# Context statistics kept for a second layer, and the order of slots in self-attention, in a transformer block on one core

## The chip, the cores and the metric

The kernel runs on one core of a Trainium2 chip. Its engines are TensorE (PE, with weight loads shown apart as PEld), VectorE (DVE), ScalarE (ACT), GpSimd (POOL) and SyncE (SP); SP, ACT and POOL also issue DMAs. The metric is the device time of one execution in microseconds. Everything is float32.

## What is computed

Two layers of a diffusion transformer (B = 8 sequences of N = 512 tokens, width H = 512, 16 heads of 32, a context of S = 77 rows for each sequence, a condition vector for each). Layer 0 is cross-attention with adaptive LayerNorm on both sides; layer 1 is self-attention with modulation, cross-attention to the same context, and an MLP:

```python
def layer_0(x, context, c):
    xq  = ada_ln(x,       c, Wss_q,  bss_q,  eps=1e-5)   # (1 + scale) * LN(x) + bias
    xkv = ada_ln(context, c, Wss_kv, bss_kv, eps=1e-5)
    return x + attention(xq @ Wq + bq, xkv @ Wkv + bkv) @ Wp + bp

def layer_1(x, context, c):
    shift_a, scale_a, gate_a, shift_m, scale_m, gate_m = split(silu(c) @ W_mod + b_mod, 6)
    q, k, v = split(modulate(ln(x), shift_a, scale_a) @ W_qkv + b_qkv, 3)
    x = x + gate_a * (softmax(q @ k.T * scale) @ v @ W_proj + b_proj)
    q_c = ln(x) @ W_qc + b_qc                            # ln: eps=1e-6
    k_c, v_c = split(ln(context) @ W_kvc + b_kvc, 2)
    x = x + softmax(q_c @ k_c.T * scale) @ v_c @ W_cproj + b_cproj
    h = gelu(modulate(ln(x), shift_m, scale_m) @ W_mlp1 + b_mlp1) @ W_mlp2 + b_mlp2
    return x + gate_m * h
```

Both layers normalise the same context rows; the mean and the variance of a row are the same in both, and only eps differs (1e-5 and 1e-6).

## The kernel before, in words

The stages follow each other: a set-up with the condition's modulations and the context's keys and values (0 to about 75 us of the profile), layer 0's cross-attention (tiles with the suffix _x, to about 450), self-attention (_a, to about 1375), layer 1's cross-attention (_c, to about 1750) and the MLP. The products of cross-attention and MLP are done in Strassen's manner, with sums of blocks on DVE and POOL.

**Context.** The 8 x 77 = 616 rows lie in CT = 5 tiles of 128 rows (the last has 104). `context_x` takes bn_stats and bn_aggr for each tile, gets 1/sqrt(var + eps) by a bit trick and Newton steps on DVE (`rsqrt`, L210 to L219), and normalises. For layer 1 the class `ContextC` loads the rows again (`load`), and its generator `norm` takes the statistics again (L428 to L432), then `rsqrt`, then normalises on ACT (L237). `transpose` makes cT_c on PE (L448) with two evacuations on ACT for each of four blocks (L452, L453); `values(t)` makes the value rows of tile t (cv_c, L345, L350) and stores them to DRAM (cvd_c) by SP; `keys(j)` makes ckT_c (L474, L479).

**Set-up.** `mod_half` makes half of a modulation: four matmuls with the silu of the condition, an ACT copy, then four transpositions on PE and an addition of the bias, which lies in a column of bcol. The bias columns come from one transposition of a table of bias rows (bcol_ps), with a copy and three scalings on DVE.

**Self-attention.** 32 groups run one after the other: batch b by fc = 0 to 3, each with four heads. A group's scores are kept transposed (keys on partitions) in four slots k = 0 to 3 of two halves, e[k][0] and e[k][1], each 128 x 1024. The steps of a group:

- `scores(k)`: eight matmuls into two PSUM tiles (sT_a, L992); for each half an ACT copy to e (L1010) and, for k > 0, a DVE maximum into mx (L1012). ACT copies half i while DVE takes the maximum of the other half, so each of them waits for the other's release of PSUM.
- `maxima()`: DVE turns mx in 32 x 32 blocks and reduces (tu_a L1023, part_a L1024, four times).
- `spread()`: PE transposes part (mxT, L1032), DVE reduces and negates (L1036), SP stores the row of maxima to DRAM (mxd).
- `shift(k)`: two DMAs on POOL's queue, 512 KB each, which broadcast mxd over the partitions and add it to e[k] (L1046).
- `exp(k)`: two ACT exponentials (L1055), each when its DMA has landed. `add_up(k)` sums e over k (L1062; on POOL, for k = 3 on DVE). `outputs(k)` multiplies by the values (o_ps, L1072). `total` and `finish` make the softmax's denominator (z_ps, L1083), its reciprocal (rz, L1090) and the product (oT, L1093).

The order is written out by hand in the loop of `self_phase`. Iteration n handles three groups: prev (n − 1), whose last slots are finished, g (n), which is shifted and begun, and nxt (n + 1), whose scores are made. Between them `pump(f[i], ...)` issues projections of the batch before (`project`, L291, followed by DVE's res_a L961 and POOL's L964 and L965), queries, keys and values of this batch or the next. The sequence before is: prev.outputs(1), nxt.scores(0), g.spread, past.total and finish, prev.add_up(2), the eight shifts with prev.exp(3) after the first two, f[0], nxt.scores(1), prev.outputs(2), f[1], nxt.scores(2), prev.add_up(3), prev.outputs(3), g.exp(0), f[2] with nxt.scores(3) in its middle, g.exp(1), g.add_up(1), nxt.maxima, g.outputs(0), f[3], g.exp(2).

In iterations with fc = 2 the next batch's normalised rows are transposed: `transpose_x(b + 1, t)`, t = 0 to 3, four PE transpositions (lnT, L913) and an ACT evacuation with modulation (xnT, L915) each. Before, they stand ahead of prev.outputs(2), behind it, ahead of nxt.scores(2) and behind it. load_x (L901, ACT's queue) loads the rows of the batch after the next.

The last batch (b = 7) has no next one. In its iteration with fc = 1 the context rows are loaded again; with fc = 2 (group 30 is g, group 31 is nxt) `norm` takes its statistics after nxt.scores(1) and its rsqrt after prev.add_up(3); the normalisation, `transpose`, the values and the keys stand in the code behind the loop, among group 31's shift, exponentials and outputs, as do the loads of x_c (the first rows of the next phase, `next_x`), of the gate and of the residual rows (`load_tile`), the statistics of x_c (`rows`), and the last batch's projection.

Of the kernel before, what the change touches and what calls it, by code (L numbers as in the profile page):

```python
# [11 lines left out]
F32 = mybir.dt.float32  # L12
# [17 lines left out]
def tile_pixart_block(ctx: ExitStack, tc: tile.TileContext, a: dict, out: bass.AP):  # L30
# [6 lines left out]
    MC = MLP // P  # L37

# [46 lines left out]

    def mod_half(u, w, bname, dst, pool, psp, tag):
# [8 lines left out]
        mark = nc.scalar.copy(m, ps[:B, :])  # L95
        pt = psp.tile([P, H], F32, tag=tag, name=f"modT_ps_{bname}_{u}")
# [12 lines left out]

    R = B * S  # L110
    CT = -(-R // P)
    RL = R - (CT - 1) * P

# [32 lines left out]
    with tc.tile_pool(name="setup_ps", bufs=2, space=PSUM) as spp:  # L146
# [17 lines left out]

        bp = spp.tile([P, H], F32, tag="ps", name="bcol_ps")
# [8 lines left out]
        w_ss_kv = [load_w("L0_xcond_Wss_kv", u) for u in range(2)]  # L174
        for u in range(2):
            mark = mod_half(u, w_ss_kv[u], "L0_xcond_bss_kv", mod_kv, sp, spp, "ps")
# [119 lines left out]
    def run(gen):  # L296
        while True:
            try:
                next(gen)
            except StopIteration as stop:  # L300
                return stop.value

# [32 lines left out]
    with tc.tile_pool(name="ps_s", bufs=2, space=PSUM, reuse_waits="tile") as ps_s:  # L335
# [17 lines left out]
        def context_x(eps, w_k, w_v, bkv, work, prep, cx):  # L353
# [14 lines left out]
            for k in range(KC):  # L368
# [14 lines left out]
                if k % 2:  # L383
                    mark = mod_half(k // 2, w_ss_q[k // 2], "L0_xcond_bss_q", mod_q, prep, ps_m, "m")
# [20 lines left out]
            return kT, vs, last, mark  # L405

        class ContextC:
# [17 lines left out]
            def norm(self):  # L425

                mv = small.tile([P, CT, 2], F32, tag="cmv", bufs=1, name="cmv_c")
                nc.vector.memset(mv, 1.0)  # L428
                for t, n in enumerate(parts):
                    bn = small.tile([P, 6], F32, tag="st", name=f"cst_c_{t}")  # L430
                    nc.vector.bn_stats(bn[:n], self.cx[t][:n])
# [448 lines left out]
        def self_phase(w, bo_row, work, work_2, ctx_c):  # L880
# [93 lines left out]
            class Group:  # L974
# [78 lines left out]
                def exp(self, k):  # L1053
                    for i in range(2):
# [74 lines left out]
            for n, g in enumerate(groups[:-1]):  # L1129
# [3 lines left out]
                f = beside(b, fc)  # L1133
                if fc == 3:
# [27 lines left out]
                if fc == 3 or (b, fc) == (0, 0) or fc == 2 and not more:  # L1162
# [16 lines left out]
                if fc == 2 and more:  # L1179
                    transpose_x(b + 1, 2)  # L1180
                nxt.scores(2)
                if fc == 2 and more:
# [3 lines left out]
                if prev is not None:  # L1186
                    prev.add_up(3)
                if (b, fc) == (0, 0) or fc == 2 and not more:
                    next(ln)
                if prev is not None:  # L1190
                    prev.outputs(3)
# [38 lines left out]
            run(ctx_c.values(1))  # L1230
# [403 lines left out]
```

## Time and profile before

| | us |
|---|---|
| median of 3 runs | 2559.84 (2558.33 to 2559.86) |
| the profiled execution | 2562.95 |
| its span in the profile | 2561.1 |
| granted TensorE clock, mean | 0.988 of full speed |

Shares of the chain of work that ended last, followed back from the last instruction, by engine:

| engine | share |
|---|---|
| PE | 31% |
| issue (waiting for nothing that the profile shows) | 28% |
| DMA | 15% |
| DVE | 14% |
| POOL | 7% |
| ACT | 4% |

The page cuts the span in 40 slices of 64 us. In the slices of self-attention (from the eighth to the twenty-second) the 16 DMA engines are busy for eight or nine tenths most of the time and move about 180 to 215 GB/s; before and after they are mostly under half busy. POOL's queue (q0), which is nearly all shifts, moves 151 MB, the queues of SP and ACT (q1) 108 MB.

In a line of a group or a timeline, the name left of the arrow is what is written, right of it what is read. Brackets at the end of a timeline line give the time for which the engine had been idle, and what ended it.

### The profile page before, as it was taken

The numbers are of one execution on the slowest core, as the hardware profiler recorded it, in microseconds if no ns is written. First come the engines' busy times: TensorE is split into PE (matmuls) and PEld (weight loads), VectorE is DVE, ScalarE is ACT, GpSimd is POOL, SyncE is SP. The second block draws the span as 40 slices with busy tenths as digits, with TensorE's granted clock in tenths as the row PEclk, the third lists the DMA queues.
The fourth block names the chain that finished last, engine by engine and source line by source line (L and its number), as shares of the span: only waits on it lengthen the run. The fifth ranks groups of instructions, "written<-read, shape, count | busy, mean of one in ns | idle before, by whom it ended". The sixth has DMA issues, their size and how long they took to land.

```text
span 2561.1 us, 35366 instructions
## 1 busy us (share of the span) xinstructions
PE 2431.1 (95%) x13205; PEld 1561.8 (61%) x13205; DVE 1781.2 (70%) x3240; ACT 1222.7 (48%) x2083; POOL 1111.6 (43%) x982
## 2 busy tenths in 40 slices
PE   7899999989999999999969999998999999999998
PEld 3577776323333333333325777777888888888887
DVE  3688886478788787887766788887546545555553
ACT  1566664477676676777643666662121121121220
POOL 2245453276776877768663445445102102012011
PEclk9999999999999999999989999999999999999999
DMA  7324323589999999999985223133111011011010
GB/s 259 134 51 97 85 32 69 111 177 187 197 179 204 185 196 195 183 198 176 216 181 189 79 38 62 23 51 111 35 36 38 31 40 38 25 32 51 19 35 25
DMA packets 116676, 273.44 MB, mean 107 GB/s; under 512 B 12722, under 2 KB 29186, under 8 KB 116378
## 3 DMA queue, kind: packets, MB, share of 16 engines
q0 software_dynamic: 46368, 151.06, 32.8%
q1 hardware_dynamic: 64197, 108.37, 12.6%
q10 hardware_dynamic: 5941, 11.76, 1.3%
q8 instruction: 104, 1.70, 0.3%
q14 instruction: 66, 0.54, 0.1%
HBM read 234.78 MB, written 44.76 MB: 109 GB/s over the span
## 4 chain that ended last, share of the span: by engine, by line
PE 31%; issue 28%; DMA 15%; DVE 14%; POOL 7%; ACT 4%; POOLq 0%; SPq 0%; ACTq 0%; DVEq 0%
DMA e_a<-mxd_a 10%; PE s_ps_qx L511 4%; PE s_ps_qc L511 4%; PE s_ps_ox L511 2%; DVE mx_a L1012 2%; PE s_ps_oc L511 2%; POOL res_m L1543 2%; POOL e_a L1046 2%; DMA mxd_a<-mxT_a 2%; POOL xr L1544 2%; PE pT_ps_c L743 2%; PE pT_ps_x L743 2%; PE proj_ps_a L291 2%; DVE sum_a L1062 2%; DVE tu_a L1023 2%
## 5 line engine op out<-in xcount | busy, mean ns | idle before, releaser
L1543 POOL TENSOR_TENSOR res_m<-res_m,gate_m 128x256 f32<-128x256 f32 x64 | 52.3, 817 | 665.0 <-DVE res_m L1541 665.0
L1055 ACT ACTIVATE e_a<-e_a 128x1024 f32<-128x1024 f32 x256 | 263.4, 1056 | 108.4 <-DMA e_a<-mxd_a 107.8
L1046 POOL DMA_DIRECT2D e_a<-mxd_a x256 | 251.0, 2061 | 146.9 <-DMA mxd_a<-mxT_a 131.7
L1010 ACT COPY e_a<-sT_a 128x1024 f32<-128x1024 f32 x256 | 253.2, 1010 | 90.3 <-DVE mx_a L1012 67.1
L1477 ACT ACTIVATE hT<-hT,bcol 128x512 f32<-128x512 f32 x128 | 91.9, 722 | 237.3 <-DVE hT L1452 229.2
L1062 POOL TENSOR_TENSOR sum_a<-e_a,e_a 128x1024 f32<-128x1024 f32 x64 | 150.2, 2365 | 116.7 <-ACT e_a L1055 111.9
L992 PE MATMUL sT_a<-qT_a,kT_a 32*128 32x512 f32 x1024 | 153.6, 645 | 21.2 <-ACT e_a L1010 19.5
L1062 POOL TENSOR_TENSOR sum_a<-sum_a,e_a 128x1024 f32<-128x1024 f32 x64 | 171.2, 2686 | 2.6 <-ACT e_a L1055 1.8
L1012 DVE TENSOR_TENSOR mx_a<-sT_a,mx_a 128x1024 f32<-128x1024 f32 x128 | 150.4, 1216 | 25.7 <-PE sT_a L992 25.6
L1072 PE MATMUL o_ps_a<-e_a,v 128*32 128x512 f32 x1024 | 146.9, 618 | 13.1 <-ACT e_a L1055 13.0
L1444 PE MATMUL q_ps_h<-x_m,w_L_xcond_W_mlp 128*128 128x256 f32 x512 | 132.1, 381 | 0.0
L1444 PE MATMUL q_ps_h<-xT_m,w_L_xcond_W_mlp 128*128 128x256 f32 x512 | 131.4, 379 | 0.0
L1012 DVE TENSOR_TENSOR mx_a<-sT_a,e_a 128x1024 f32<-128x1024 f32 x64 | 77.8, 1224 | 76.9 <-PE sT_a L992 39.6
L1444 PE MATMUL q_ps_h<-x_m,w_s 128*128 128x256 f32 x512 | 122.3, 382 | 5.5 <-DVE w_s L1398 4.8
L1090 DVE RECIPROCAL rz_a<-z_ps_a 128x512 f32<-128x512 f32 x32 | 107.5, 3358 | 28.2 <-PE z_ps_a L1083 28.2
L291 PE MATMUL proj_ps_a<-w_L_xcond_W_proj,oT_a 128*128 128x512 f32 x256 | 117.6, 604 | 9.3 <-ACT xnT_a L915 9.3
L283 PE MATMUL q_ps_a<-xnT_a,w_L_xcond_W_qkv 128*128 128x512 f32 x256 | 124.1, 613 | 0.0
L283 PE MATMUL k_ps_a<-xnT_a,w_L_xcond_W_qkv 128*128 128x512 f32 x256 | 121.3, 612 | 0.0
L291 PE MATMUL v_ps<-w_L_xcond_W_qkv,xnT_a 128*128 128x512 f32 x256 | 119.7, 611 | 0.0
L992 PEld LDWEIGHTS sT_a<-qT_a,kT_a 32*128 32x128 f32 x1024 | 44.0, 183 | 120.6 <-ACT e_a L1010 55.8
L1444 PE MATMUL q_ps_y<-w_L_xcond_W_mlp,h_s 128*128 128x256 f32 x512 | 113.1, 379 | 0.0
L1444 PE MATMUL q_ps_y<-w_L_xcond_W_mlp,hT 128*128 128x256 f32 x512 | 113.1, 379 | 0.0
(370 smaller groups left out, 5574.6 us busy)
## 6 DMA issues: line engine op xcount, KB each, us to landing
e_a<-mxd_a POOLq DMA_DIRECT2D x256, 512.0 KB, 11.6
xa<-res_x POOLq DMA_DIRECT2D x32, 256.0 KB, 5.2
xr_a<-xa SPq DMA_DIRECT2D x32, 256.0 KB, 4.4
xc<-xr_a SPq DMA_DIRECT2D x32, 256.0 KB, 8.4
x_c<-xc SPq DMA_DIRECT2D x8, 1024.0 KB, 5.1
w_L_xcond_W_mlp<-in_L_xcond_W_mlp_dram SPq DMA_DIRECT2D x8, 1024.0 KB, 6.9
xc<-res_c POOLq DMA_DIRECT2D x32, 256.0 KB, 5.1
x_m<-xc SPq DMA_DIRECT2D x8, 1024.0 KB, 5.2
```

What stands on the lines that cost most here:

```text
L283: nc.tensor.matmul(ps, lhsT=w[:, k, ts(j, P)], rhs=xT[k], start=(k == 0), stop=(k == KC - 1))
L291: nc.tensor.matmul(ps, lhsT=xT[k][:, cols], rhs=w[:, k, :], start=(k == 0), stop=(k == KC - 1))
L511: nc.tensor.matmul(ps, lhsT=self.lhs[i][:, k], rhs=self.rhs[i][:, k], start=(k == 0), stop=(k == 1),)
L992: nc.tensor.matmul(sc[h // 2][:, h % 2, :], lhsT=kT[ts(h, HD), ts(k, P)], rhs=qT[ts(h, HD), :], start=True, stop=True,)
L1010: nc.scalar.copy(self.e[k][i], sc[i])
L1012: nc.vector.tensor_tensor(self.mx[1 - i], sc[1 - i], self.e[0][1 - i] if k == 1 else self.mx[1 - i], ALU.max,)
L1046: nc.gpsimd.dma_start(out=self.e[k][i].rearrange("p h n -> p (h n)"), in_=self.mxd[2 * i : 2 * i + 2, :] .rearrange("h n -> (h n)").partit ...
L1055: nc.scalar.activation(self.e[k][i], self.e[k][i], AF.Exp)
L1062: engine.tensor_tensor(sum_i, self.e[0][i] if k == 1 else sum_i, self.e[k][i], ALU.add)
L1072: nc.tensor.matmul(self.po[ts(h, HD), :], lhsT=vt[:, self.fc * P + h * HD : self.fc * P + (h + 1) * HD], rhs=self.e[k][h // 2][:, h % 2, : ...
L1090: nc.vector.reciprocal(r, self.pz)
L1444: nc.tensor.matmul(self.banks[n][:, half], lhsT=lhsT, rhs=rhs, start=(k == 0), stop=(k == len(pairs) - 1),)
```

## The change

- The mean and variance of the context's rows, as layer 0 took them (`mv`), are handed from `context_x` to `ContextC`, which makes the factor (with eps 1e-6) and the offset from them when it is built, ahead of the self-attention phase: a rsqrt, a copy and an offset on tiles of 128 x 5. The memset, bn_stats, bn_aggr and the rsqrt in the last loop iteration go.
- Two of the five context tiles are normalised after nxt.scores(2) of the last iteration, three after g.exp(1); `transpose` stands at that iteration's end, ahead of the last group's first step.
- Behind the loop the values, the keys, the loads of x_c, gate and residual rows, and x_c's statistics take other places among the last group's slots.
- prev.exp(3) is split: its first half stays, its second half goes behind nxt.scores(1) (and behind the first transposition of a turning iteration).
- The transpositions of a turning iteration take other slots: 0 as before, 1 behind f[1] and ahead of nxt.scores(2), 2 behind these, 3 and load_x behind prev.outputs(3).
- `mod_half` becomes a generator that pauses after its ACT copy; the bias table's transposition, copy and scalings come between the two parts of the first half, and w_ss_kv is loaded ahead of them.

The core of the diff (the moves of `run`, R, CT and RL to an earlier place are left out):

```diff
@@ set-up
+        w_ss_kv = [load_w("L0_xcond_Wss_kv", u) for u in range(2)]
+        halves = [
+            mod_half(u, w_ss_kv[u], "L0_xcond_bss_kv", mod_kv, sp, spp, "ps") for u in range(2)
+        ]
+        next(halves[0])
         bp = spp.tile([P, H], F32, tag="ps", name="bcol_ps")
         nc.tensor.transpose(bp[:, :n_cols], brow, ident[:n_cols, :n_cols])
...
-        for u in range(2):
-            mark = mod_half(u, w_ss_kv[u], "L0_xcond_bss_kv", mod_kv, sp, spp, "ps")
+        run(halves[0])
+        mark = run(halves[1])
@@ class ContextC
-            def __init__(self, w_v, work):
+            def __init__(self, w_v, work, mv):
+                y = rsqrt(mv[:, :, 1], 1e-6, "cc", CT)
+                self.y = small.tile([P, CT], F32, tag="cy", bufs=1, name="cy_c")
+                self.off = small.tile([P, CT], F32, tag="coff", bufs=1, name="coff_c")
+                nc.vector.tensor_copy(self.y, y)
+                nc.vector.scalar_tensor_tensor(self.off, mv[:, :, 0], -1.0, y, ALU.mult, ALU.mult)
...
             def norm(self):
-                mv = small.tile([P, CT, 2], F32, tag="cmv", bufs=1, name="cmv_c")
-                nc.vector.memset(mv, 1.0)
                 for t, n in enumerate(parts):
-                    bn = small.tile([P, 6], F32, tag="st", name=f"cst_c_{t}")
-                    nc.vector.bn_stats(bn[:n], self.cx[t][:n])
-                    nc.vector.bn_aggr(mv[:n, t, :], bn[:n])
-                    if t in (2, CT - 1):
-                        yield
-                y = rsqrt(mv[:, :, 1], 1e-6, "cc", CT)
-                off = offsets(mv, y, CT)
-                yield
-                for t, n in enumerate(parts):
-                    normalise_s(self.cx[t][:n], self.cx[t][:n], off, y, t, n)
+                    normalise_s(self.cx[t][:n], self.cx[t][:n], self.off, self.y, t, n)
+                    yield
@@ the loop of self_phase
+                turning = fc == 2 and more
...
-                    prev.exp(3)
+                    prev.exp(3, [0])
...
                 nxt.scores(1)
-                if fc == 3 or (b, fc) == (0, 0) or fc == 2 and not more:
+                if fc == 3 or (b, fc) == (0, 0):
                     next(ln, None)
                     next(ln, None)
...
-                if fc == 2 and more:
+                if turning:
                     transpose_x(b + 1, 0)
                 if prev is not None:
+                    prev.exp(3, [1])
                     prev.outputs(2)
-                if fc == 2 and more:
-                    transpose_x(b + 1, 1)
...
                 pump(f[1], 4)
...
-                if fc == 2 and more:
-                    transpose_x(b + 1, 2)
+                if turning:
+                    transpose_x(b + 1, 1)
                 nxt.scores(2)
-                if fc == 2 and more:
-                    transpose_x(b + 1, 3)
-                    if b + 2 < B:
-                        load_x(b + 2)
+                if turning:
+                    transpose_x(b + 1, 2)
+                if fc == 2 and not more:
+                    next(ln)
+                    next(ln)
                 if prev is not None:
                     prev.add_up(3)
-                if (b, fc) == (0, 0) or fc == 2 and not more:
+                if (b, fc) == (0, 0):
                     next(ln)
                 if prev is not None:
                     prev.outputs(3)
+                if turning:
+                    transpose_x(b + 1, 3)
+                    if b + 2 < B:
+                        load_x(b + 2)
...
                 g.add_up(1)
+                if fc == 2 and not more:
+                    run(ln)
                 nxt.maxima()
                 g.outputs(0)
                 pump(f[3], 4)
+                if fc == 2 and not more:
+                    ctx_c.transpose()
                 g.exp(2)
@@ behind the loop
-            run(ln)
             prev.outputs(2)
-            ctx_c.transpose()
+            for t in range(2):
+                run(ctx_c.values(t))
             prev.add_up(3)
             prev.outputs(3)
-            run(ctx_c.values(0))
+            value = ctx_c.values(2)
+            next(value)
             prev.total()
+            run(value)
             prev.finish()
...
             next_x(nc.sync)
-            run(ctx_c.values(1))
-            value = None
             rows = ln_rows("c", 0, 1e-6)
+            fills = [ctx_c.values(3), ctx_c.values(4), ctx_c.keys(0)]
             for k in range(NT):
                 g.exp(k)
                 if k:
                     g.add_up(k)
-                    run(value)
                 g.outputs(k)
-                if k == 2:
+                if k == 0:
                     st[g.b]["g"] = gate_rows(gate_a, g.b, work, "a")
-                    for _ in range(4):
-                        next(rows)
                     for t in range(NT):
                         load_tile(B - 1, t, nc.sync)
-                if k + 2 < CT:
-                    value = ctx_c.values(k + 2)
-                    next(value)
-            run(value)
-            run(rows)
+                if k < len(fills):
+                    run(fills[k])
             w_c = [load_w("L1_xcond_W_qc", 0, queue=nc.scalar)]
             w_c.append(load_w("L1_xcond_W_cproj", 0, queue=nc.scalar))
-            run(ctx_c.keys(0))
+            run(ctx_c.keys(1))
             g.total()
             g.finish()
-            run(ctx_c.keys(1))
+            run(rows)
             for t in range(NT):
                 run(project(B - 1, t))
```

More of the change, by code (lines that the diff above doesn't have):

```diff
@@ L37, in tile_pixart_block @@
     MC = MLP // P
+    R = B * S
+    CT = -(-R // P)
+    RL = R - (CT - 1) * P
     const = ctx.enter_context(tc.tile_pool(name="const", bufs=1))
@@ L84, in bias_cols, with run @@
         return bcol[:, c : c + n]
+    def run(gen):
+        while True:
+            try:
+                next(gen)
+            except StopIteration as stop:
+                return stop.value
     def mod_half(u, w, bname, dst, pool, psp, tag):
@@ L108, in mod_half @@
         return mark
-    R = B * S
-    CT = -(-R // P)
-    RL = R - (CT - 1) * P
     def load_context(pool):
@@ L172, in tile_pixart_block @@
             )
-        w_ss_kv = [load_w("L0_xcond_Wss_kv", u) for u in range(2)]
-        for u in range(2):
-            mark = mod_half(u, w_ss_kv[u], "L0_xcond_bss_kv", mod_kv, sp, spp, "ps")
+        run(halves[0])
+        mark = run(halves[1])
         w_ss_q = [load_w("L0_xcond_Wss_q", 0)]
@@ L294, in mm_N @@
             yield
[L296 to L301, printed above, removed]
     def gate_rows(gate, b, pool, nm, bufs=2):
@@ L383, in context_x @@
                 if k % 2:
-                    mark = mod_half(k // 2, w_ss_q[k // 2], "L0_xcond_bss_q", mod_q, prep, ps_m, "m")
+                    mark = run(mod_half(k // 2, w_ss_q[k // 2], "L0_xcond_bss_q", mod_q, prep, ps_m, "m"))
             vd = dram.tile([R, H], F32, name="cvd_x")
@@ L404, in context_x @@
             prep.release()
-            return kT, vs, last, mark
+            return kT, vs, last, mark, mv
         class ContextC:
-            def __init__(self, w_v, work):
+            def __init__(self, w_v, work, mv):
[4 more added lines that the diff above has]
+                nc.vector.scalar_tensor_tensor(self.off, mv[:, :, 0], -1.0, y, ALU.mult, ALU.mult)
                 self.work, self.w_v = work, w_v
@@ L425, in norm @@
             def norm(self):
-                mv = small.tile([P, CT, 2], F32, tag="cmv", bufs=1, name="cmv_c")
-                nc.vector.memset(mv, 1.0)
                 for t, n in enumerate(parts):
-                    bn = small.tile([P, 6], F32, tag="st", name=f"cst_c_{t}")
-                    nc.vector.bn_stats(bn[:n], self.cx[t][:n])
-                    nc.vector.bn_aggr(mv[:n, t, :], bn[:n])
-                    if t in (2, CT - 1):
-                        yield
-                y = rsqrt(mv[:, :, 1], 1e-6, "cc", CT)
-                off = offsets(mv, y, CT)
-                yield
-                for t, n in enumerate(parts):
-                    normalise_s(self.cx[t][:n], self.cx[t][:n], off, y, t, n)
+                    normalise_s(self.cx[t][:n], self.cx[t][:n], self.off, self.y, t, n)
+                    yield
             def transpose(self):
@@ L1051, in shift, with exp @@
                         )
-                def exp(self, k):
-                    for i in range(2):
+                def exp(self, k, halves=(0, 1)):
+                    for i in halves:
                         nc.scalar.activation(self.e[k][i], self.e[k][i], AF.Exp)
@@ L1178, in self_phase @@
                     ln = ctx_c.norm()
-                if fc == 2 and more:
+                if turning:
+                    transpose_x(b + 1, 1)
+                nxt.scores(2)
+                if turning:
                     transpose_x(b + 1, 2)
-                nxt.scores(2)
-                if fc == 2 and more:
+                if fc == 2 and not more:
+                    next(ln)
+                    next(ln)
+                if prev is not None:
+                    prev.add_up(3)
+                if (b, fc) == (0, 0):
+                    next(ln)
+                if prev is not None:
+                    prev.outputs(3)
+                if turning:
                     transpose_x(b + 1, 3)
@@ L1185, in self_phase @@
                         load_x(b + 2)
-                if prev is not None:
-                    prev.add_up(3)
-                if (b, fc) == (0, 0) or fc == 2 and not more:
-                    next(ln)
-                if prev is not None:
-                    prev.outputs(3)
                 flush(0)
@@ L1314, in tile_pixart_block @@
             with tc.manual_schedule(engines={ENG.PE}):
-                kT, vs, last, mark = context_x(1e-5, w_l0[0], w_l0[1], names[1], kv_x, sp, cx)
+                kT, vs, last, mark, c_mv = context_x(1e-5, w_l0[0], w_l0[1], names[1], kv_x, sp, cx)
             stack.enter_context(tc.manual_schedule(engines=ALL_BUT_SYNC))
@@ L1334, in tile_pixart_block @@
             w_l1 = [load_w("L1_xcond_W_qkv", u) for u in (2, 0, 1)] + [load_w("L1_xcond_W_proj", 0)]
-            ctx_c = ContextC(load_w("L1_xcond_W_kvc", 1), work)
+            ctx_c = ContextC(load_w("L1_xcond_W_kvc", 1), work, c_mv)
             w_c, kv = self_phase(w_l1, load_row("L1_xcond_b_proj", 0, "bo"), work, work_2, ctx_c)
```

## The prediction

> **What bounds the kernel now.** I read the page first, then TensorE's and ACT's waits in the self-attention loop, then the engines' shares by stretch, then the timeline at the loop's end.
>
> ```profile
> PE 2431.1 (95%) x13205; PEld 1561.8 (61%) x13205; DVE 1781.2 (70%) x3240; ACT 1222.7 (48%) x2083; POOL 1111.6 (43%) x982
> ...
> L1055 ACT ACTIVATE e_a<-e_a 128x1024 f32<-128x1024 f32 x256 | 263.4, 1056 | 108.4 <-DMA e_a<-mxd_a 107.8
> L1046 POOL DMA_DIRECT2D e_a<-mxd_a x256 | 251.0, 2061 | 146.9 <-DMA mxd_a<-mxT_a 131.7
> ```
>
> TensorE is busy for 95% of the span, so only its 130 us of idle time, and what it does twice, can be won. Much of that idle time is in the self-attention phase (450 to 1375 us). Its waits from 450 to 1350 us (engine, line, what it waited for: us, times, longest):
>
> ```profile
> PE mxT_ps_a L1032 <- DVE part_a L1024: 20.3, 25, 2.7
> PE sT_a L992 <- ACT e_a L1010: 19.5, 17, 4.7
> PE o_ps_a L1072 <- ACT e_a L1055: 13.0, 3, 10.2
> PE proj_ps_a L291 <- ACT xnT_a L915: 9.3, 6, 2.4
> ```
>
> The third is nearly all one wait, at the loop's end; the others are spread over the groups. A turning group (fc 2, where the next batch is transposed) shows the second and fourth kinds: ACT stands in e[3]'s second half until its transfer lands, and the score copies and the evacuation that the projection needs queue up behind it. ACT, then TensorE:
>
> ```profile
> 752.48 1.06 ACT L1055 ACTIVATE e_a<-e_a 128x1024 f32<-128x1024 f32 x1 [1.24 <-DMA e_a<-mxd_a]
> 753.44 1.91 ACT L1010 COPY e_a<-sT_a 128x1024 f32<-128x1024 f32 x2
> ```
> ```profile
> 756.09 3.70 PE L291 MATMUL proj_ps_a<-w_L_xcond_W_proj,oT_a 128*128 128x512 f32 x8 [1.02 <-ACT xnT_a L915]
> ...
> 775.83 0.30 PE L1032 MATMUL mxT_ps_a<-ident,part_a 128*64 128x128 f32 x1 [1.17 <-DVE part_a L1024]
> ```
>
> A second resource stands close behind TensorE. By stretch (length, PE, PEld, DVE, ACT, POOL busy, granted clock, DMA share, GB/s):
>
> ```profile
> 680.00:860.00 180.00, 170.94 (x743) 56.37 (x742) 150.99 (x182) 127.13 (x145) 130.68 (x93) 1.00 0.95 192
> 860.00:1040.00 180.00, 170.62 (x746) 56.89 (x748) 148.39 (x178) 126.53 (x143) 135.92 (x98) 1.00 0.96 195
> ```
>
> PE idles 9 us in 180 (5%), the DMA engines 4 to 5%. Neither can give more than some 40 us over the loop's 790 us. The loop's end, DVE, then PE, then POOL:
>
> ```profile
> 1288.08 0.68 DVE L431 BATCH_NORM_STATS2 cst_c<-cx 128x6 f32<-128x512 f32 x1
> ...
> 1298.26 1.23 DVE L210 TENSOR_SCALAR lnv_cc<-cmv_c 128x5 f32<-128x5 f32 x1
> ...
> 1305.74 2.35 DVE L1012 TENSOR_TENSOR mx_a<-sT_a,mx_a 128x1024 f32<-128x1024 f32 x2
> ```
> ```profile
> 1295.03 1.76 PE L992 MATMUL sT_a<-qT_a,kT_a 32*128 32x512 f32 x8 [4.71 <-ACT e_a L1010]
> ...
> 1309.07 2.87 PE L1072 MATMUL o_ps_a<-e_a,v 128*32 128x512 f32 x8 [10.22 <-ACT e_a L1055]
> 1313.88 0.30 PE L1032 MATMUL mxT_ps_a<-ident,part_a 128*64 128x128 f32 x1 [1.94 <-DVE part_a L1024]
> ```
> ```profile
> 1316.48 1.79 POOL L1046 DMA_DIRECT2D e_a<-mxd_a  x2 [2.69 <-DMA mxd_a<-mxT_a]
> ```
>
> Context statistics hold the scores' maxima of the last group; ACT's score copy waits for those, and the exponentials wait behind the copy: 4.71 + 10.22 + 1.94 us of TensorE.
>
> **Statistics once, and the last slots.** Removed from DVE in the last loop iteration: 1288.08 to 1292.15 = 4.1 us (five bn_stats and bn_aggr) and 1298.26 to 1305.83 = 7.5 us (13 small operations, up to 1.23 us each beside POOL's adds, 0.17 without). So the maxima end up to 11.6 us sooner: mx2 from 1289.1 (sT2 is there then), 2.35 us, the sums 3.4, mx3 2.35, four transposes with reduces 5.7: part ready near 1303 for 1313.9. But the 20 context transpositions now stand ahead of mxT(31) on PE, and their last three inputs are normalised (3 x 0.72 us) after exp(1), whose transfer lands at 1299.57 and which ends near 1300.6; transpositions and eight evacuations take 3.5 us more: about 1306.5 for mxT(31). (The evacuations hold up exp(2), landed at 1304.87, by some 1.6 us; o(30,2) and o(30,3) wait for the last landing anyway.) mxd goes out near 1307, and group 30's transfers drain at 1311.27; so the first shift of group 31 goes from 1316.48 to about 1312, a gain of 4.4 us. TensorE's idle time of 16.9 us isn't the gain: group 31 can't start before the queue of group 30 drains. The rest turns into waiting for that.
> On SP two more value stores (cvd_c1, cvd_c2) now go ahead of x_c0, and the gate and xr loads ahead of cvd_c3; these loads (x_c0 1 MB, four xr rows 1 MB) share some 8 us more of group 31's transfers. From 1330 to 1342, queue 0 moved 1.84 MB beside queue 1's 1.02 (153 KB/us); successive landings without queue 1 (1299.57, 1302.05) give 512 KB in 2.5 us, about 200: 8 x 47/200 = +1.8 us. The stretch 1318 to 1328 without queue 1 shows only 168 KB/us, which makes it +0.7; I take 1.8.
> The Trainium skill ("DMA: Bandwidth & Descriptors", section "Queues, rings and completion order") says that each engine takes the queues in turn, a packet from each; with the 4 KB and 2 KB packets here that is an estimate of two thirds for queue 0, and 8 x 1/3 = +2.7 us in place of +1.8. The row's 153 of 200 is kinder than the rule.
> After the last landing (before: 1345.73) the order saves PE's 2.48 us wait for z at 1354.90, and moves one value block and ckT0 (4.5 us, 1347.85 to 1352.3) under the transfers; x_c's statistics (5.7 us on DVE) go ahead of the residual instead: the end of the projection comes 25.3 us after the landing, for 28.5 (1374.21 − 1345.73): −3.2. Tail: −4.4 + 1.8 − 3.2 = **−5.9** (rounded), between −9 (no sharing) and −2 (mxT late by 4 us more).
>
> **What that adds earlier.** 14 small DVE operations come into the first cross phase near 383 to 388 us, ten ahead of u_qx (L637 at 385.24). Alone 0.17 us, 0.2 apart: 10 x 0.2 = 2 us, less 0.46 us of slack before s_x and part of the 0.86 us that DVE idles at 388.07: **+0.9**. Low end 0 (slack covers it). High end: beside POOL's adds 13 took 7.5 us, but POOL runs two adds of 0.72 us here: +2.5.
> The skill's "SBUF — State Buffer" (section "Who interferes with whom") says that a vector operation with two SBUF inputs waits for a whole GpSimd instruction that reads SBUF; the row agrees in kind (0.17 against 1.23 us). By this rule each of the ten could wait out an add of 0.72 us, an estimate of 7.2 − 1.3 = +6; what no run here shows is whether every one would meet an add.
>
> **Setup.** The bias transposition moves from 12.84 us, in a shadow (csT's copy waits for statistics of cx), into the gap of the ACT copy that feeds modT (PE idle 0.67 us from 20.73): 0.42 us of it hides there, its DVE copy of 0.25 doesn't quite: **+0.1**; −0.9 if the later bp row lets cx land sooner, +1 if the modT addition slips behind DVE's normalisation.
>
> **Half an exponential, turning order.** ACT no longer waits for the transfer's last landing ahead of sT1's copies. Of PE's sT_a waits 4.71 and 0.5 belong to the tail; 14.3 us are the loop's. The projection's 9.3 us go, since lnT0's evacuation has o2 and no landing ahead of it. In turning groups the maxima start about 1.5 us sooner, and mxT's wait (1.17 at 775.83) falls to about 0.2: 7 x 1.0 = 7. Added: xnT_2 stands behind two score copies of 1.01 us; with lnT2, o3 and lnT3 (2.4 us) as cover its q waits up to 0.65 us, 7 times: 4.5. Net 14.3 + 9.3 + 7 − 4.5 = 26 us of PE waits. PE then meets the next thing sooner: the group's landings, which follow mxT by mxd and the transfers (longest piece of the chain from 700 to 840 us: transfers, 39%). Where each side has 5% of slack I halve it: **−13**. Low end −20 (three quarters), high end 0 (below). load_x moves some 2 us later, with a whole group as cover, and add_up(3) gets its second half about 3 us later while DVE takes it 8 us after (702.25 to 711.65): nothing.
>
> **Sum** against the profiled execution (2562.95 us, of which span 2561.1): −13 − 5.9 + 0.9 + 0.1 = −17.9, so 2545. That execution lies 3.1 us over the median of 2559.84; against the median: **2542**, its own range 2536 to 2548 (loop −7 to −19).
>
> **Rivals.**
> *Transfers set the loop's pace.* For: DMA share 0.95; mxd takes 5 to 7 us (776.48, 7.16 us) beside full queues, and shifts follow soon after the previous group's last landing. Against: after that landing the first of the next needs 4.9 us (1316.48 to 1321.43), so an earlier mxT fills a hole. Loop 0: −5.9 + 1 = −4.9, **2555**.
> *The half does nothing* (ACT waits at e[3]'s first half or e[2] instead; only part of 77 waits at L1055 are the last landing). Only turning: (9.3 + 7 − 4.5)/2 = −6; total −10.9, **2549**.
> *Turning stalls at q.* xnT_2 and xnT_3 wait behind sT2's second copy, and that waits for DVE's maximum. For: ACT's copies waited for it 67.1 us in 68 waits. Against: at 761.38 both came within 0.34 us. At 3.9 us, as at 1293.96, less 0.7 of cover: 7 x 3.2 = +22, less the half's −7, less the tail with additions −4.9: +10, **2570**; it makes the kernel slower from 1.7 us per turn beyond that cover.
>
> **Chances.** Forecast 0.47, half does nothing 0.21, transfers 0.18, turning stall 0.11, something else 0.03. A measurement here tells 0.2% (5.1 us) from no change. Faster: 0.47 + 0.21 + 0.08 of the transfers' case = 0.76; same 0.13; slower 0.11. Range 2531 (loop −20, tail −9, half a microsecond spent elsewhere) to 2558 (transfers' case with tail −2); the stall is left out.
>
> **What will show it.** Right: the DVE stretch at 1288 to 1306 without L431 and L210; no PE wait of 10 us there; first shift of group 31 a few us after group 30's last landing; PE's waits sT_a under 8 us and xnT_a near 0; loop 1.9 us shorter per batch. Wrong: PE waits the same in sum, with o_ps_a or mxT_ps_a grown (transfers); a new q_ps_a wait for xnT_a over 1.7 us (stall); or a gap in the first cross phase near 385 us.

## The result, and the profile after

The changed kernel takes 2553.69 us (median of 18 runs, 2547.21 to 2558.03), the kernel before 2560.66 (18 runs, 2557.71 to 2565.1): a ratio of 0.9971, 95% interval 0.9963 to 0.9978, or 7.4 us less (5.6 to 9.5). The forecast was 18 us less. The rival in which the transfers set the loop's pace stood at 4.9 us less.

TensorE's waits from 450 to 1350 us in the changed kernel (engine, line, what it waited for: us, times, longest):

```profile
PE sT_a L991 <- ACT e_a L1009: 16.1, 17, 2.8
PE o_ps_a L1071 <- ACT e_a L1054: 12.8, 10, 2.0
PE mxT_ps_a L1031 <- DVE part_a L1023: 11.3, 18, 2.7
PE q_ps_a L294 <- ACT xnT_a L914: 7.6, 7, 1.4
PE cT_ps_c L447 <- ACT cx L248: 4.0, 3, 3.5
```

The 10.2 us wait at the loop's end is gone, and so are the projection's waits for xnT_a. But the sum of the main waits fell only from 62.1 to 51.8 us: nearly as many short ones came in other places (q_ps for xnT_a, o_ps for the exponentials, cT for cx). The other half of the picture is POOL, in the same stretch, first before, then after:

```profile
POOL e_a L1046 <- DMA mxd_a<-mxT_a: 131.7, 27, 38.4
```
```profile
POOL e_a L1045 <- DMA mxd_a<-mxT_a: 148.6, 28, 38.4
```

POOL stands 17 us longer before the shifts, waiting for the row of maxima to land in DRAM. One turning group shows what that means. The kernel before, TensorE and then POOL; then the changed kernel, likewise:

```profile
671.16 0.30 PE L1032 MATMUL mxT_ps_a<-ident,part_a 128*64 128x128 f32 x1 [1.17 <-DVE part_a L1024]
```
```profile
678.46 1.79 POOL L1046 DMA_DIRECT2D e_a<-mxd_a  x2 [4.49 <-DMA mxd_a<-mxT_a]
```
```profile
666.85 0.30 PE L1031 MATMUL mxT_ps_a<-ident,part_a 128*64 128x128 f32 x1
```
```profile
676.76 1.79 POOL L1045 DMA_DIRECT2D e_a<-mxd_a  x2 [5.15 <-DMA mxd_a<-mxT_a]
```

The maxima are transposed 4.3 us sooner, without a wait; the shift starts 1.7 us sooner. It starts 0.46 us after the last landing of the group before (676.30) where it started 0.76 after it (677.70). So in this group the shift follows the landing, not the transposition.

The trace gives for each group the issue of its first shift, the landing of its last, and the issue of its mxd store. From these the loop from group 0's last landing to group 30's splits, with no rest, into transfer times (first shift issued to last landing) and gaps (last landing to the next group's first shift). The lead is the time by which mxd is issued ahead of the previous group's last landing. "Tail" is from group 30's last landing to group 31's, "end" from there to the end of the last projection. All in us, from one profiled execution each, groups 1 to 30; the ratio is that of the timed runs to the kernel before.

| kernel | loop | transfers | gaps | mean lead | tail | end | ratio (95%) |
|---|---|---|---|---|---|---|---|
| before | 794.1 | 779.1 | 14.9 | 5.2 | 34.5 | 28.6 | 1 |
| changed | 790.1 | 780.5 | 9.6 | 6.0 | 30.3 | 28.9 | 0.9971 (0.9963–0.9978) |
| u_loop | 791.8 | 776.9 | 14.9 | 4.8 | 30.9 | 28.8 | 0.9981 (0.9972–0.9990) |
| l_only | 789.8 | 778.2 | 11.5 | 5.9 | 31.2 | 29.4 | 0.9977 (0.9969–0.9986) |
| half_only | 791.4 | 779.2 | 12.2 | 5.8 | 32.4 | 31.9* | 0.9980 (0.9972–0.9989) |
| turn_only | 792.1 | 778.9 | 13.3 | 5.8 | 33.9 | 32.1* | 1.0002 (0.9993–1.0011) |
| stat_only | 793.7 | 776.7 | 17.1 | 5.2 | 29.1 | 29.9 | 0.9988 (0.9979–0.9997) |
| x_pe | 796.0 | 773.3 | 22.6 | 4.4 | 30.9 | 28.5 | 1.0001 (0.9993–1.0010) |
| x_less | 761.4 | 695.7 | 65.7 | 0.7 | | | 0.9842 (0.9828–0.9855) |
| y_shift | 796.0 | 776.5 | 19.5 | 3.9 | 27.9 | 31.9 | 0.9989 (0.9978–1.0000) |
| z_exp | 856.4 | 773.1 | 83.2 | −0.2 | 30.6 | 31.9 | 1.0239 (1.0224–1.0253) |
| z_half | 797.1 | 784.8 | 12.3 | 5.0 | 29.4 | 33.2 | 0.9999 (0.9991–1.0008) |
| y_tail | 790.0 | 778.8 | 11.2 | 6.0 | 30.1 | 24.7 | 0.9947 (0.9934–0.9960) |
| y_late | 787.7 | 777.1 | 10.7 | 5.9 | 30.0 | 24.6 | 0.9952 (0.9939–0.9966) |

The star marks a granted clock of 0.89 in that stretch, 1.00 in the others. The kernels changed, y_tail and y_late are alike up to group 30's transfers, and their loops took 790.1, 790.0 and 787.7 us: a difference of some 2 us between two rows tells nothing. Differences between two edited kernels are taken below from their ratios, since the kernel before was timed afresh beside each batch (medians 2560.66 to 2563.18); by the medians they are up to 2 us different (u_loop 3.7 us above the changed kernel for 2.6, x_pe 9.5 for 7.7, x_less 31.4 below it for 33, y_tail 5.1 for 6.1).

Between the profiled executions of before and after, the time went so: up to group 0's last landing +1.3, loop −4.0, tail −4.1, end +0.3, the rest +0.5 (cross-attention and MLP, which the change leaves alone): −6.1 of span. Of the loop's −4.0, 1.9 us is a single gap of 2.6 us in group 1 of the profile before.

The granted clock differs too. Its mean over the execution was 0.990 in the changed kernel's 18 runs and 0.986 in the 27 runs of the kernel before that stand beside turn_only; among the runs of either kernel the time falls by about 1 us for each 0.001 of it. So some 4 of the 7.4 us go along with a higher clock. Whether the change raised it, by sparing TensorE long waits, is not shown; z_exp below bears on it.

### The profile page after: what moved, and what is told of

Same layout as the page of the kernel before. It is cut to its first block, busy times and chain, and to the rows that moved or that the text cites. A ratio compares the mean times of both kernels' runs of the same rounds, so it can differ in the third digit from the quotient of the medians.

```text
span 2555.1 us, 35387 instructions
## 1 busy us (share of the span) xinstructions
PE 2437.6 (95%) x13205; PEld 1562.6 (61%) x13205; DVE 1776.1 (70%) x3230; ACT 1224.9 (48%) x2083; POOL 1103.1 (43%) x982
## 5 line engine op out<-in xcount | busy, mean ns | idle before, releaser
L1011 DVE TENSOR_TENSOR mx_a<-sT_a,mx_a 128x1024 f32<-128x1024 f32 x128 | 150.9, 1216 | 33.6 <-PE sT_a L991 27.9
L991 PE MATMUL sT_a<-qT_a,kT_a 32*128 32x512 f32 x1024 | 151.4, 640 | 17.7 <-ACT e_a L1009 16.1
L1071 PE MATMUL o_ps_a<-e_a,v 128*32 128x512 f32 x1024 | 152.9, 608 | 12.8 <-ACT e_a L1054 12.8
L1089 DVE RECIPROCAL rz_a<-z_ps_a 128x512 f32<-128x512 f32 x32 | 107.4, 3357 | 31.9 <-PE z_ps_a L1082 31.9
L1447 PE MATMUL q_ps_y<-w_t,h_s 128*128 128x256 f32 x512 | 111.8, 379 | 0.0
```

Source lines behind the costliest of these rows:

```text
L991: nc.tensor.matmul(sc[h // 2][:, h % 2, :], lhsT=kT[ts(h, HD), ts(k, P)], rhs=qT[ts(h, HD), :], start=True, stop=True,)
L1011: nc.vector.tensor_tensor(self.mx[1 - i], sc[1 - i], self.e[0][1 - i] if k == 1 else self.mx[1 - i], ALU.max,)
L1071: nc.tensor.matmul(self.po[ts(h, HD), :], lhsT=vt[:, self.fc * P + h * HD : self.fc * P + (h + 1) * HD], rhs=self.e[k][h // 2][:, h % 2, : ...
L1089: nc.vector.reciprocal(r, self.pz)
L1447: nc.tensor.matmul(self.banks[n][:, half], lhsT=lhsT, rhs=rhs, start=(k == 0), stop=(k == len(pairs) - 1),)
```

## The experiments

Theory T says that the shifts' transfers set the loop's pace, theory P (the forecast) that TensorE's chain with its waits does.

**u_loop: the loop's two parts undone.**

```diff
-                    prev.exp(3, [0])
+                    prev.exp(3)
...
-                    prev.exp(3, [1])
                     prev.outputs(2)
+                if turning:
+                    transpose_x(b + 1, 1)
...
-                if turning:
-                    transpose_x(b + 1, 1)
+                if turning:
+                    transpose_x(b + 1, 2)
                 nxt.scores(2)
-                if turning:
-                    transpose_x(b + 1, 2)
+                if turning:
+                    transpose_x(b + 1, 3)
+                    if b + 2 < B:
+                        load_x(b + 2)
```

> The changed kernel with the loop's two parts undone (the half exponential and the order of the turning transpositions are as before); the statistics, the tail's order and the set-up stay changed. Theory T (the shifts' transfers set the loop's pace): the loop from the first group's last landing to group 30's takes what it takes in the changed kernel, within 3 us, and the total is 0 to 3 us above the changed kernel's 2553.7. Theory P (TensorE's chain sets the pace, as forecast): 10 to 15 us above it, 2564 to 2569.

Measured: 0.9981 of the kernel before, for the changed kernel's 0.9971: 2.6 us above it, by the ratios. The loop took 1.7 us longer. That is T's number (by the medians, 3.7 us, it would lie just above T's 0 to 3); P's 10 to 15 us are excluded by the intervals.

**x_pe: more TensorE work.**

```diff
-                    for h in range(4):
+                    for h in (0, 1, 2, 3) * (2 if k == 1 else 1):
                         nc.tensor.matmul(
```

> The changed kernel with the score matmuls of slot 1 issued twice in every group: 32 x 1.14 = 36 us more TensorE work in the loop, with no other effect. T: mxT's lead over the previous group's last landing shrinks by 1.1 us a group and most of it is not seen: 0 to 10 us more than the changed kernel, shifts still within 1 us of the last landing. P: 25 to 36 us more.

Measured: ratio 1.0001, 7.7 us above the changed kernel. The added work is less than the 36 us expected: sixteen score matmuls in a row hold TensorE for 1.93 us where eight hold it for 1.07, so 32 x 0.86 = some 28 us. In the loop TensorE's idle time fell from 44.6 to 32.1 us. The mean lead fell from 6.0 to 4.4 us, the gaps rose from 9.6 to 22.6 us in sum, and the transfers fell by 7. TensorE had some 0.6 us a group to give away. T, within its range, though not free.

**x_less: one transfer in eight left out.**

```diff
-                    for i in range(2):
+                    for i in range(k == 2, 2):
                         nc.gpsimd.dma_start(
```

> The changed kernel without the shift of e[2][0] (one of eight transfers of 512 KB a group is left out, so that half is not lowered by its maximum ahead of the exponential, and its softmax is not the reference's). TensorE's work, the last landing's place in the order and the exponentials stay. T: 2.5 us less of transfer a group, until TensorE bounds the loop, which idles 43 us there: 25 to 45 us less than the changed kernel. P: 0 to 5 us less.

Measured: 0.9842, 33 us below the changed kernel; the loop took 28.6 us less. (Some 5 us lie ahead of group 0's first shift: from 425 to 450 us the granted clock is 1.00 in this profile, 0.80 in the changed kernel's. The profiles of y_shift, z_exp and z_half have the same 1.00, and start the loop as early.) This is the one edit that buys what TensorE's idle time had seemed to offer. By stretch, the columns as in the prediction, TensorE is now busy 177.10 of 180 us, where it was 173.14 in the changed kernel, and the DMA share falls from 0.97 to 0.88; the changed kernel, then x_less:

```profile
860.00:1040.00 180.00, 173.14 (x744) 57.17 (x743) 149.15 (x177) 127.64 (x143) 134.65 (x96) 1.00 0.97 198
```
```profile
860.00:1040.00 180.00, 177.10 (x778) 57.90 (x780) 152.66 (x188) 134.11 (x151) 129.23 (x90) 1.00 0.88 180
```

The loop's bound has moved: the mean lead is 0.7 us and the gaps 2.2 us a group, so here the transfers wait for TensorE. P, with at most 5 us, is refuted; T holds until this bound.

**y_shift: two more transfers ahead of POOL's sum** (for the last group likewise).

```diff
                 g.shift(0)
+                g.shift(1)
                 if prev is not None:
                     prev.add_up(2, [1])
...
-                for k in range(1, NT):
+                for k in range(2, NT):
                     g.shift(k)
```

> The changed kernel with the shift of slot 1 issued ahead of the sum add_up(2, [1]) on the POOL queue, so that two more transfers are queued before POOL turns to the 3 us sum. In the changed kernel the third landing of a group comes some 3.5 us after the second, where 2.5 us is usual. T: up to 1 us a group, 15 to 30 us less than the changed kernel, unless the sum, now later, holds up the exponentials' sums. P: no change within 3 us.

A miss of T, which forecast 15 to 30 us less: 0.9989, 4.6 us above the changed kernel. The third landing did come 2.5 us after the second (group 20: 9.4 and 11.9 us after the first shift), but the second came 9.4 us after the first shift instead of 8.1. A group's transfers took 25.9 us for 26.0. The late third landing had been no hole in the transfers. The sum now starts 1.1 us later after the first shift and ends 1.8 us later, and the lead is 3.9 us for 6.0; that the sum cost this lead is likely, not shown, since the loop's granted clock was also lower in this profile (0.98 for 0.99).

**l_only, half_only, turn_only: the loop's parts alone, on the kernel before.** The edits are the reverse of u_loop's, both together and each alone.

> The kernel before with the loop's two parts alone (the half exponential and the order of the turning transpositions); statistics, tail and set-up as before. Theory T (the shifts' transfers set the loop's pace): 0 to 4 us less than the kernel before, and the last landings of successive groups as far apart as before. Theory P (TensorE's chain sets the pace): 10 to 15 us less than the kernel before.

> The kernel before with the half exponential alone. Theory T (transfers set the loop's pace): TensorE's waits for the score copies fall, and the time by 0 to 3 us. Theory P: 5 to 8 us less.

> The kernel before with the turning transpositions' order alone. T: the projection's waits for xnT_a go, and the time falls by 0 to 3 us. P: 4 to 7 us less.

Measured: 0.9977 together, 0.9980 for the half exponential, 1.0002 for the turning order. P fails for both together (5.9 us less, 3.6 to 7.9 by the interval, for its 10 to 15) and for the turning order. For the half exponential it does not fail by its size: 5.1 us less (2.8 to 7.2) reaches into P's 5 to 8 and lies above T's 0 to 3, so this run alone does not decide. T's sizes were short for the first two. The profiles put only a part of this in the loop: the half exponential acts in the last iteration too, where it cuts the tail from 34.5 to 32.4 us, besides the loop's 2.7. The turning order, which took away the projection's 9.3 us of waits and raised the lead of the next group (fc 3) from 5.7 to 7.4 us, is worth nothing that these runs can tell from zero (−1.8 to +2.8 us). Other waits came in their place here too (6.2 us of the queries' projection for xnT_a, the scores' 25.5 for 19.5), and TensorE's idle time in the loop fell by 4.7 us only (56.5 to 51.8).

**stat_only: the statistics once, all else as before.**

```diff
             def norm(self):
-                mv = small.tile([P, CT, 2], F32, tag="cmv", bufs=1, name="cmv_c")
...
-                y = rsqrt(mv[:, :, 1], 1e-6, "cc", CT)
-                off = offsets(mv, y, CT)
-                yield
+                for _ in range(3):
+                    yield
                 for t, n in enumerate(parts):
-                    normalise_s(self.cx[t][:n], self.cx[t][:n], off, y, t, n)
+                    normalise_s(self.cx[t][:n], self.cx[t][:n], self.off, self.y, t, n)
```

> The kernel before with the context statistics alone taken once (factor and offset made ahead of self-attention; normalisation, transpositions, values, keys and loads stay in their old places). If freeing DVE is what the tail gained, group 31's last landing comes 30 to 31.5 us after group 30's, for 34.5 before, and the time is 2 to 5 us under the kernel before's. If the order of the last slots gained it, nothing changes within 2 us.

Measured (ContextC is built as in the changed kernel): 0.9988 (3.1 us less), tail 29.1 us. Freeing DVE is what shortened the tail; the new order of the last slots added nothing to it (30.3 in the changed kernel). u_loop's 4.9 us and l_only's 5.9 make 10.8, but both together gave 7.4: a shortfall of 3.4 us that the intervals just allow as noise, and that the tail explains if it is real, since both shorten the same tail (to 30.9 and 31.2 us alone, to 30.3 together).

**z_exp: the half exponential one slot further on.**

```diff
-                    prev.exp(3, [1])
                     prev.outputs(2)
...
                 nxt.scores(2)
+                if prev is not None:
+                    prev.exp(3, [1])
```

> The changed kernel with the second half of exp(3) moved on, from behind slot 1's score copies to behind slot 2's, so that two more copies no longer wait for the group's last landing. Theory T1 (the loop goes from last landing to last landing; mxd's landing comes 0.7 us after the last landing unless mxd is issued over 6 us ahead of it): mxT comes 1 to 2 us earlier, shifts go from 0.7 us after to about the last landing, 5 to 20 us less than the changed kernel. Theory T2 (mxd lands with the last landing however early it is issued): within 3 us.

A miss of both theories: 61 us slower than the kernel before. TensorE's waits in this kernel:

```profile
PE o_ps_a L1071 <- ACT e_a L1054: 66.5, 30, 2.4
```

In every group outputs(3), which follows scores(2) on TensorE (a transposition stands between them in turning iterations), waits 2.2 us for an exponential that now stands behind two copies of 1.01 us. TensorE becomes the bound: mxd leaves when the queue has already drained (lead −0.2 us), and the gaps grow to 2.8 us a group. The loop got 66 us longer. These waits came in place of others, so only half of that is idle time: TensorE's rose from 44.6 us in the changed kernel's loop to 77.7, and its busy time rose as much, from 745.4 to 778.7, for about as many matmuls (3217 for 3233) at a lower granted clock (0.96 for 0.99). The clock fell to 0.50 in 16 pieces of 3.4 us or more, each beginning within 4 us of the start of a wait of over 1.5 us; from 578.10 to 581.30, say, right behind a wait of 2.45 us, it is 0.50. Only two such pieces lie in the changed kernel's loop. So a wait of TensorE seems to cost its length and slower work behind it; that the wait brings the lower clock is read from their places, and no run tests it. x_pe's work comes when the landing is still ahead, this wait after it; that the place makes the difference is argued, not shown.

**z_half: the maxima in two halves.** Heads 2 and 3 are turned, transposed and stored ahead of heads 0 and 1, and each shift takes its second half first; some small tiles get two buffers for it. The moves in the loop:

```diff
-                nxt.maxima()
+                nxt.maxima(1)
                 g.outputs(0)
                 pump(f[3], 4)
...
                 g.exp(2)
+                nxt.spread(1)
+                nxt.maxima(0)
                 past, prev = prev, g
```

> The changed kernel with the maxima spread in two halves: heads 2 and 3 are turned, transposed on PE and stored to DRAM as soon as they are reduced, ahead of the turns of heads 0 and 1; every shift takes its second half first. The first store leaves some 2 us earlier than the changed kernel's one store. T1: the first shift of a group goes some 1 to 2 us earlier against the last landing, 10 to 30 us less than the changed kernel, until TensorE bounds the loop. T2: within 3 us, or slower by the added transposition and store (some 0.6 us of PE and DVE a group).

T1's gain is missed: 0.9999, 7.2 us above the changed kernel, which T2 had allowed for. But the first store left no sooner (a lead of 5.0 us for the single store's 6.0), since TensorE now met the transposition ahead of its input:

```profile
PE mxT_ps_a L1033 <- DVE part_a L1026: 46.7, 37, 3.3
```

So it says nothing on whether an earlier store would land earlier.

**y_tail and y_late: the last slots in another order.** In y_tail ckT0's evacuation goes behind exp(3), z ahead of ckT1, and x_c's statistics ahead of the reciprocal:

```diff
-            fills = [ctx_c.values(3), ctx_c.values(4), ctx_c.keys(0)]
+            fills = [ctx_c.values(3), ctx_c.values(4)]
+            key_0 = ctx_c.keys(0)
...
+                elif k == 2:
+                    pump(key_0, KC)
...
-            run(ctx_c.keys(1))
+            run(key_0)
             g.total()
+            for _ in range(2):
+                next(rows)
             g.finish()
+            run(ctx_c.keys(1))
             run(rows)
```

> The changed kernel with another order behind the last group's exponentials: ckT0's evacuation behind exp(3) instead of ahead of it (its first four matmuls stay ahead of outputs(3)), z ahead of ckT1, x_c's statistics on DVE ahead of the reciprocal. If the tail's lost 3 us sit in ckT0's evacuation and in the residual behind x_c's statistics, the projection ends 24 to 26 us after the last landing instead of 28.9, and the time is 3 to 5 us under the changed kernel's. If something else holds the projection, nothing changes within 2 us.

Measured: the projection ends 24.7 us after the last landing, and the ratio is 0.9947: 6.1 us below the changed kernel (3 to 5 were expected), 13.6 below the kernel before. The changed kernel's lines, ACT and then TensorE, and y_tail's TensorE:

```profile
1340.56 0.69 ACT L478 ACTIVATE ckT_c<-ckT_ps_c,bcol 128x512 f32<-128x512 f32 x1 [4.78 <-PE ckT_ps_c L473]
...
1341.68 1.05 ACT L1054 ACTIVATE e_a<-e_a 128x1024 f32<-128x1024 f32 x1
```
```profile
1342.78 2.00 PE L1071 MATMUL o_ps_a<-e_a,v 128*32 128x512 f32 x8 [1.38 <-ACT e_a L1054]
...
1354.48 4.56 PE L302 MATMUL proj_ps_a<-w_L_xcond_W_proj,oT_a 128*128 128x512 f32 x10 [1.43 <-DVE oT_a L1092]
1360.72 7.13 PE L302 MATMUL proj_ps_a<-w_L_xcond_W_proj,oT_a 128*128 128x512 f32 x16 [1.68 <-DVE res_a L960]
```
```profile
1340.04 1.07 PE L1071 MATMUL o_ps_a<-e_a,v 128*32 128x512 f32 x8
...
1348.93 13.92 PE L302 MATMUL proj_ps_a<-w_L_xcond_W_proj,oT_a 128*128 128x512 f32 x32
```

In the changed kernel the last two exponentials stand behind ckT0's evacuation, which waits for TensorE: they start at 1341.68, though the last transfer landed at 1338.92. In y_tail the projection runs its 13.9 us through.

In y_late the gate's and the residual rows' loads are issued after the loop over the last group's slots instead of in its first pass.

```diff
-                if k == 0:
-                    st[g.b]["g"] = gate_rows(gate_a, g.b, work, "a")
-                    for t in range(NT):
-                        load_tile(B - 1, t, nc.sync)
...
+            st[g.b]["g"] = gate_rows(gate_a, g.b, work, "a")
+            for t in range(NT):
+                load_tile(B - 1, t, nc.sync)
             w_c = [load_w("L1_xcond_W_qc", 0, queue=nc.scalar)]
```

> The kernel y_tail (the changed kernel with its last slots put in another order) with the gate's and the four residual rows' loads issued behind group 31's transfers instead of beside them. If these 1.25 MB slow group 31's transfers as queue 1's share of 153 to 200 KB/us says, the last landing comes 2 to 3.5 us sooner and the time is 1 to 3 us under y_tail's; if the residual additions then wait for their rows, nothing is gained or up to 3 us lost.

Measured: 0.9952, not to be told from y_tail; the tail is 30.0 us for 30.1. This doesn't show that such loads are free. Between group 30's and group 31's last landings q1 (SP's loads and stores; the loads that ACT issues run on q10) moved 2.21 MB in y_tail and 2.26 in y_late: the stores of the values and the load of x_c stand ahead in both. In y_tail the first residual rows landed at 1339.69, after the last transfer (1338.19), so the edit took next to nothing away from beside the transfers.

## Why the prediction was wrong, point by point

**The loop, −13 (range −20 to 0): this is the step that failed.** The prediction counted 26 us of TensorE's waits and put half of them down as time, because "each side has 5% of slack". Two of its three waits went as foreseen (xnT_a's for the projection gone, mxT's from 20.3 to 11.3 us). The largest, 14.3 us of the scores' waits for their copies, did not: they fell from 19.5 to 16.1, not under 8. But TensorE's idle time wasn't slack to be won: the loop is the sum of the groups' transfers, which stay at 773 to 785 us in every kernel with all eight transfers, and of gaps, which were 14.9 us in all and fell to 9.6. The −13 would have needed nearly every gap closed; they gave 5.3 us, and the transfers took 1.4 back. The DMA share of 0.95 said that the transfers nearly abut; the prediction read its missing 5% as room. x_less shows the bound from the one side (33 us for a transfer less), x_pe from the other (7.7 us for some 28 us more TensorE work). The loop gave 4.0 us in the profiles, 2.6 by u_loop's ratio. This was the prediction's own rival, held at 0.18. Its mechanism was right; that its sum of −4.9 lies near the measured −7.4 is partly luck, since it had 0 for the loop's −4.0 and took over a tail of −5.9 that came to −3.8 with the end.

Its objection to that rival was that "an earlier mxT fills a hole", the 4.9 us from a first shift to its landing. That hole is real, but an earlier mxT hardly reaches it: with leads of 7.5 us (fc 3) the first shift still came at most 1.2 us ahead of the last landing, and on average 0.2 after it.

**The tail, −4.4 + 1.8.** The gap ahead of group 31 fell from 5.2 to 0.6 us (−4.6, right). Group 31's transfers took 29.7 us for 29.3, with 2.45 MB on q1 beside them for 1.93: +0.5 instead of +1.8, so the bound from the other row, +0.7, was the better one. The row from 1330 to 1342 us was misread, too: queue 0 had 1.84 of 2.86 MB in it, 64%, so it agrees with the two thirds that the prediction works out from the Trainium skill ("DMA: Bandwidth & Descriptors", section "Queues, rings and completion order"); but the sum of both queues was 238 KB/us, more than the 200 of queue 0 alone. Together −4.1 for −2.6. (Two sums are slightly off, without effect: −4.4 + 1.8 − 3.2 is −5.8, and the top of the range, the transfers' case with its +1, is 2559.)

**Behind the last landing, −3.2: failed.** It gave +0.3. The prediction let ckT0 lie "under the transfers" without counting that its evacuation stands ahead of the last two exponentials on ACT. The cover ended 2.5 us before the work did: the last transfer landed at 1338.92, ckT0 ended at 1341.4 on TensorE. And x_c's statistics, 5.7 us on DVE ahead of the residual, held the projection's third tile by 1.68 us. y_tail, which takes out these two (and puts z ahead of ckT1), gets −4.3 against the changed kernel: the −3.2 was there to be had by another order.

**The hoisted statistics, +0.9: too much.** From the last projection but one ahead of s_x to the next transposition on TensorE it takes 3.94 us with them (385.07 to 389.01), 3.88 without (384.09 to 387.97). On DVE u_qx came 0.85 us later against these marks, which s_x's slack took up: +0.06. The +6 by the rule that the prediction cites (the Trainium skill, "SBUF — State Buffer", section "Who interferes with whom") didn't come: all 14 operations took 0.15 to 0.17 us. That doesn't refute the rule, since they hardly met POOL's two additions. An older operation with two SBUF inputs (lnt_a, L229) began at 385.37 in the addition from 385.31 to 386.05, and took 0.70 us. The prediction's own row is a mixed one: of its five long operations the first two (L210 and L212, 1.23 and 1.19 us) have a single input.

**The set-up, +0.1: about right.** From the first modulation matmul to its transposition it takes 5.96 us in u_loop, which has the new set-up, and 5.94 before. In the changed kernel's own profile it is 6.54, of which 0.59 are longer matmuls. The rest of the 1.3 us by which group 0 landed later in it is not explained by the two terms; from 75 to 100 us the granted clock was 0.86 in it, 1.00 before.

**Turning stalls at q** (0.11): the wait came, 7.6 us in 7 waits, the longest 1.4. That is more than the forecast's 4.5 us and far less than this rival's 3.2 us each, and by turn_only it made nothing slower that can be told. **The half does nothing** (0.21) was wrong the other way round: the half exponential is the loop part that tells, the turning order the one that doesn't.

## What to carry to other kernels

Where a loop is paced by transfers, split it into transfer time and gaps, group by group, before costing an edit on an engine: only the gaps can be won, however many waits the engine shows. A share of 0.95 on the DMA engines with back-to-back groups was the bound here, and the test is cheap: add work to the busy engine, take a transfer away. Work that is laid under a transfer brings its evacuations with it, in the queue of the engine that must answer the transfer's landing.

## What the runs showed of the hardware

The 8 KB store of maxima lands in 1.7 us from its issue when the shifts' queue is empty (z_exp, 824.29 to 825.95, the previous group's last landing being 823.26). Beside queued shifts it lands about when they do: 8.5 us after its issue in the changed kernel (773.06 to 781.58, the previous group's last landing being 781.42). Over twelve of the kernels (without x_less and z_half), 177 groups have a lead between 1.5 and 5.5 us: the median gap is 0.70 us, and in 137 of them it lies between 0.6 and 0.8. With over 6 us (118 groups) the median gap is 0.31 us, and the shift comes at most 2.3 us ahead of the last landing. The Trainium skill ("DMA: Bandwidth & Descriptors", section "Queues, rings and completion order") says that a semaphore's increment lands only after every earlier write of that DMA engine, across its queues. That agrees in kind with the 8.5 against 1.7 us; no run here tells whether the store's data or only its increment is late. Whether a store with a lead of 10 us or more would open the next group's transfers ahead of the last landing wasn't tried; z_half, meant to do it, gained no lead.
